# Expert rows that carry their norm, probability and token number, and a scatter from each expert tile to the output

## The chip, the cores and the metric

The kernel runs on one core of a Trainium2 chip. The metric is device time in microseconds of one execution, from the runs listed below. The core has five instruction streams that this text names as the profile does: PE (TensorE, matrix products, with PEld for its weight loads), DVE (VectorE), ACT (ScalarE), POOL (GpSimd) and SP (SyncE, which here only issues DMAs). Each stream works off its instructions in a fixed order; an instruction that waits holds up everything behind it on the same stream. SBUF is the on-chip memory of 128 partitions, PSUM the memory that matmuls write to, and HBM the memory outside.

## The reference

Four batches of 512 tokens of width 128 pass through four residual layers: `x + mamba/attention block`, `x + gelu MLP with ternary weights`, `x + mamba block`, and `x + mixture of experts`. Only the last one is touched. In it, with the layer norm of `x` as its input:

```
logits = x @ router_w + router_b
route = jax.nn.softmax(logits, axis=1)
max_prob = jnp.max(route, axis=1, keepdims=True)
max_ind = jnp.argmax(route, axis=1)
for e in range(num_experts):            # 8 experts
    h = x @ w1[e]                       # 128 -> 2 x 512
    a, g = jnp.split(h, 2, axis=1)
    y = jax.nn.silu(a) * g @ w2[e]      # 512 -> 128
    out = jnp.where((max_ind == e)[:, None], y, out)
out = out * max_prob
```

Every token thus needs one expert only, the one with the largest logit; its output is multiplied by that expert's probability and added to the token's residual.

## The kernel before

The work on a batch is cut into generators: fronts (norm, convolution, projections), scans (the state recurrences of a mamba layer, 16 jobs of two states each), `first` (attention), `dense` (two MLPs), `second` (`back1` and `route`), `sort`, `experts` and `collect`. The function `run` gives each a due time and a length, and `issue` draws one step of whichever is due next; this is the order in which the instructions are written down. A scheduler then fixes the order on each engine by its own estimate of when each is ready, and places the semaphores. Two helpers bind it further: `behind` lets something be issued only after a given instruction, and `when` adds a true dependency. A buffer tag with `bufs=n` has n buffers in rotation; a tile waits until all users of the buffer's last tile are done.

**The scans.** In `scan_states` each job makes two rows of B in PSUM (PE, L455), two decays (ACT, L459), two products and two scans (DVE, L495 and L496), and a product of 128x1024 with the loaded rows `rep` on POOL (L497); PE adds its result up in `y` (L480). The transfers `rep` go through SP's queue (L464). The instruction `self.product` is the latest of POOL's products.

**Route.** `route` (L679) normalises a batch for the experts: moments on DVE, the factor `r` on POOL (`rstd`, L292), the offset `nm_r` on DVE and the normalised rows on ACT (`shifted`, L310), which go to a tile of tag `h`. It computes logits, the one-hot choice `hot`, and the probability `top` of the chosen expert (L719).

**Sort.** Batches go through the experts in two groups, (0, 1) and (2, 3), each of 1024 tokens. `sort` (L721) counts the tokens of each expert with matmuls, and gives each token a position `posi` in an HBM buffer `sorted`, in which every expert's rows start at a multiple of 128. The buffer has 15 tiles of 128 rows, enough for any distribution, and is filled with zeros in the setup (L218 to L229). Eight indirect DMAs on POOL (L770), one for each 128 tokens, put the normalised rows there. `owni` says which expert owns each tile.

**Experts.** `experts` (L780) runs over the 15 tiles of its group. `load(j)` reads a tile `xg` from `sorted` (SP, after all eight puts), the expert's number into a register, and its weights `w_up` (512 KB, two buffers) and `w_dn` (256 KB, three) from HBM; it transposes the rows on PE (`tp`, L799) and copies them to `xj` on ACT (L801). The step of tile j then makes eight matmuls (`a_ps` L820 and `g_ps` L827), SiLU on ACT (L824) and the product on DVE (L830). `down(j - 1)` makes the four down matmuls of the previous tile (`w_ps`, L807), copies the result to `yj` on ACT (L812) and stores it through SP's queue to an HBM buffer `back` (L813). After it comes `load(j + 1)`.

**Collect.** `collect` (L841) brings one batch back in token order: four indirect DMAs on POOL gather its rows from `back` into `acc` (L848; held behind POOL's latest scan product), two POOL instructions multiply by `top` and add the residual `x` (L852 and L853), and SP stores the batch (L854). `acc` has a single buffer. Due times put the collects of batches 0 and 1 shortly after the last scan, those of 2 and 3 at the end.

Of the kernel before, what the change touches and what calls it, by code (L numbers as in the profile page):

```python
# [18 lines left out]
P = 128  # L19
# [13 lines left out]
NXR = NR + E - 1  # L33
NG = 2
SCALE = HD ** -0.5
NEG = -1e30
# [15 lines left out]
class Net:  # L52


    def __init__(self, ctx, tc, a, out):
        self.tc, self.nc, self.a, self.out = tc, tc.nc, a, out
        pool = lambda name, bufs, **k: ctx.enter_context(tc.tile_pool(name=name, bufs=bufs, **k))
        self.const = pool("const", 1)
        self.tok = pool("tok", 2)
        self.feat = pool("feat", 2)  # L60
        self.scan = pool("scan", 2)
        self.small = pool("small", 2)
        self.p_mm = pool("p_mm", 4, space=PSUM)
        self.p_b = pool("p_b", 3, space=PSUM)
        self.p_y = pool("p_y", 1, space=PSUM)
        self.dram = pool("dram", 2, space=DRAM)
        self.x = [None] * B

# [86 lines left out]
    def setup_rest(self):  # L155
# [5 lines left out]
        nc.gpsimd.tensor_copy(self.ident_b, self.ident)  # L161
        self.ones = self.c("ones", [P, P])
        nc.gpsimd.memset(self.ones, 1.0)
# [41 lines left out]
        )  # L205
        self.ones_b = self.c("ones_b", [P, P], BF16)
        nc.gpsimd.memset(self.ones_b, 1.0)
# [9 lines left out]
        )  # L217
        zero = self.big("zero", [P, NX, D])  # L218
        nc.gpsimd.memset(zero, 0.0)
        self.sorted = []  # L220
        for k, rows in enumerate(GROUPS):
            n = len(rows) * NT + E - 1
            d = self.dram.tile([n * P, D], F32, tag=f"sorted{k}", name=f"sorted{k}", bufs=1)
            for j in range(0, n, NX):
                m = min(NX, n - j)
                nc.sync.dma_start(
                    out=d[j * P:(j + m) * P, :].rearrange("(j p) d -> p j d", p=P), in_=zero[:, :m, :]
                )
            self.sorted.append(d)  # L229
# [38 lines left out]
    def ternary(self, name, raw, shape):  # L268

        nc = self.nc  # L270
        col = self.c(f"abs_{name}", [P, 1])
        nc.vector.tensor_reduce(
            col, raw, AX.X if len(shape) == 2 else AX.XY, ALU.add, apply_absolute_value=True
        )
        ps = self.mm(f"abs_ps_{name}")
        nc.tensor.matmul(ps[:, 0:1], lhsT=self.ones, rhs=col, start=True, stop=True)
        thr = self.c(f"thr_{name}", [P, 1])
        nc.vector.tensor_scalar(thr, ps[:, 0:1], 0.5 / (D * HID), 0.5e-6, ALU.mult, ALU.add)
        nthr = self.c(f"nthr_{name}", [P, 1])
        nc.vector.tensor_scalar(nthr, thr, -1.0, None, ALU.mult)  # L280
        low = self.big(f"low_{name}", shape)
        nc.vector.tensor_scalar(low, raw, nthr, None, ALU.is_lt)
        w = self.c(f"tern_{name}", shape)
        nc.vector.scalar_tensor_tensor(w, raw, thr, low, ALU.is_gt, ALU.subtract)
        return w

    def load_x(self, b):
        self.x[b] = self.tok.tile([P, NT, D], F32, tag="x", name=f"x_{b}", bufs=B)
        self.nc.sync.dma_start(out=self.x[b], in_=self.a["x"][b].rearrange("(t p) d -> p t d", p=P))


    def rstd(self, name, var, eps):  # L292
        nc = self.nc
        r = self.sm("r", [P, NT], bufs=4)
        ve = self.sm("ve", [P, NT], bufs=4)
        nc.gpsimd.tensor_scalar(ve, var, eps, None, ALU.add)
        nc.gpsimd.tensor_tensor(r, ve, self.nhalf, ALU.pow)
        return r
# [10 lines left out]

    def shifted(self, y, x, mean, r, name="nm_r"):  # L310

        nc = self.nc
        off = self.sm(name, [P, NT], bufs=4)
        nc.vector.scalar_tensor_tensor(off, mean, -1.0, r, ALU.mult, ALU.mult)
# [49 lines left out]
    def front(self, b, layer, x, scale=None):  # L364
# [53 lines left out]
        du = self.ft("du", [P, NB, T])  # L418
        v, e = self.ft("sp_v", [P, NB, T], bufs=1), self.ft("sp_e", [P, NB, T], bufs=1)
        for c in range(NB):  # L420
# [20 lines left out]
    def scan_states(self, b, layer):  # L441
# [47 lines left out]
        for k, (c, n) in enumerate(jobs):  # L489
# [4 lines left out]
            for i, b in enumerate(b_n):  # L494
                nc.vector.tensor_tensor(b, b, du[:, c, :], ALU.mult)  # L495
                nc.vector.tensor_tensor_scan(hs[:, i, :], da[:, i, :], b, 0.0, ALU.mult, ALU.add)  # L496
            self.product = nc.gpsimd.tensor_tensor(hs, hs, rep, ALU.mult)  # L497
            done[k] = hs
# [180 lines left out]
    def route(self, b):  # L679
# [4 lines left out]
        if n == 0:  # L684
            self.choice = (
                self.sm("hot", [P, NR, E], bufs=1)[:, :nr],
                self.small.tile([P, NR, E], BF16, tag="hot_b", name="hot_b", bufs=1)[:, :nr],
                self.sm("top", [P, NR])[:, :nr],
            )
        hot, hb, top = (t[:, ts] for t in self.choice)  # L690
        x = self.x[b]
        mv = self.moments("e", [x[:, t, :] for t in range(NT)])
        ln = self.shifted(self.t4("h", bufs=4), x, mv[:, :, 0], self.rstd("e", mv[:, :, 1], 1e-5))
        self.h[b] = ln
        xT = self.transposed(ln)
# [22 lines left out]
        nc.vector.tensor_reduce(sum_e, lg, AX.X, ALU.add)  # L718
        nc.vector.reciprocal(top, sum_e)  # L719

    def sort(self, group):  # L721
        nc = self.nc
        hot, hb, top = self.choice
        nr = len(group) * NT
# [4 lines left out]
        for s in range(1, nr):  # L729
            nc.tensor.matmul(  # L730
                rk[:, s:, :], lhsT=self.ones_b, rhs=hb[:, :nr - s, :], start=False, stop=(s == nr - 1)
            )
        ct = self.mm("count_ps")[:, :E]
        for t in range(nr):
            nc.tensor.matmul(ct, lhsT=self.ones_b, rhs=hb[:, t, :], start=(t == 0), stop=(t == nr - 1))

# [32 lines left out]
        for t in range(nr):  # L769
            put = nc.gpsimd.indirect_dma_start(  # L770
                out=srt, out_offset=bass.IndirectOffsetOnAxis(ap=posi[:, t:t + 1].bitcast(U32), axis=0),
                in_=self.h[group[t // NT]][:, t % NT, :], in_offset=None,
            )
# [3 lines left out]
        yield  # L777
        self.order = srt, puts, owni, posi, top

    def experts(self, group):  # L780
        nc = self.nc
        srt, puts, owni, posi, top = self.order
        nx = len(group) * NT + E - 1
        back = self.dram.tile([nx * P, D], F32, tag="back", name="back")

        def load(j):

            xg = self.ft("xg", [P, D], bufs=2)
            get = nc.sync.dma_start(out=xg, in_=srt[j * P:(j + 1) * P, :])
# [5 lines left out]
            with self.behind(self.rep):  # L795
                for part, name in zip(w, ("w1_rows", "w2_rows")):
                    nc.sync.dma_start(out=part, in_=self.a[name][bass.ds(e, 1)].rearrange("o p n -> (o p) n"))
            tp = self.mm("tp")
            nc.tensor.transpose(tp[:, :P], xg, self.ident)  # L799
            xj = self.ft("xj", [P, P])  # L800
            nc.scalar.copy(xj, tp[:, :P])  # L801
            return w, xj

        def down(j, w, sa):
            ps = self.mm("w2_ps")
            for f in range(EF // P):
# [3 lines left out]
                )  # L810
            yj = self.ft("yj", [P, D])
            nc.scalar.copy(yj, ps[:, :D])  # L812
            nc.sync.dma_start(out=back[j * P:(j + 1) * P, :], in_=yj)  # L813

        ahead, last = load(0), None
        for j in range(nx):
            w, xj = ahead
            pa = self.mm4("a_ps")
# [12 lines left out]
            if last is not None:  # L831
                down(j - 1, *last)
            last = w, sa
            if j + 1 < nx:
                ahead = load(j + 1)
            yield
        down(nx - 1, *last)
        for n, b in enumerate(group):
            self.moe[b] = back, posi[:, n * NT:(n + 1) * NT], top[:, n * NT:(n + 1) * NT]

    def collect(self, b):  # L841

        nc = self.nc
        back, posi, top = self.moe[b]
        acc = self.t4("acc", bufs=1)
        with self.behind(self.product):
            for t in range(NT):
                nc.gpsimd.indirect_dma_start(  # L848
                    out=acc[:, t, :], out_offset=None, in_=back,
                    in_offset=bass.IndirectOffsetOnAxis(ap=posi[:, t:t + 1].bitcast(U32), axis=0),  # L850
                )
        nc.gpsimd.tensor_tensor(acc, acc, top.unsqueeze(2).to_broadcast([P, NT, D]), ALU.mult)  # L852
        nc.gpsimd.tensor_tensor(acc, acc, self.x[b], ALU.add)  # L853
        nc.sync.dma_start(out=self.out[b].rearrange("(t p) d -> p t d", p=P), in_=acc)  # L854
        yield

# [13 lines left out]
    def run(self):  # L870
        self.h, self.m = [None] * B, [None] * B
        self.fronts, self.backs, self.last_head = 0, {}, None
        self.moe, self.product = [None] * B, None
        self.setup()
# [5 lines left out]
        for b in range(B):  # L880
# [6 lines left out]
            stages.append((b + B + 1, 0.1, self.second(b)))  # L887
            stages.append((2 * B + (0.2 if b in GROUPS[0] else 2), 0.1, self.collect(b)))
        for group in GROUPS:
# [5 lines left out]
def steps(g):  # L895

    return {
        "scan0": 17, "scan1": 17, "front0": 8, "front1": 8, "first": 15, "dense": 8, "second": 1,
        "sort": 1, "experts": NXR, "collect": 1, "setup_rest": 5,
    }[g.__name__]  # L900
# [70 lines left out]
```

## Time and profile before

| | us |
|---|---|
| median of 3 runs | 995.21 (995.03 to 995.97) |
| profiled execution | 998.23 |
| its span in the profile | 996.5 |

| engine | busy us of the span | share |
|---|---|---|
| PE | 806.9 | 81% |
| DVE | 654.1 | 66% |
| ACT | 563.1 | 57% |
| POOL | 455.7 | 46% |

The span runs from the first to the last event of the profile on this core. A busy share is an average over stages with different limits. Shapes are written as partitions x elements. A row of a group of instructions gives the line, the engine and operation, the names of what is written and read, then busy time and mean duration, and the idle time of the engine before it with what ended it. A row of the timeline gives start, length, engine, line, operation, names, and in brackets the engine's wait before it. Relevant sizes from the page: the 30 expert tiles (15 for each group) move 512 KB of `w_up`, 256 KB of `w_dn`, 64 KB of `xg` and 64 KB of `back` each; the 16 puts and the 16 gathers are POOL instructions of about 0.97 us each.

### The profile page before, as it was taken

What the parts mean: (1) busy time and instruction counts of PE and PEld (TensorE: products, weight loads), DVE (VectorE), ACT (ScalarE), POOL (GpSimd) and SP (SyncE); (2) the same over time, 40 slices, a digit from 0 to 9 for tenths busy, and PEclk for the clock granted to TensorE, in tenths of its full rate; (3) what the DMA queues carried; (4) which work ended last, traced back from release to release, by engine and by line L of the source; (5) the groups of instructions that cost most, each with busy time, mean ns of one, the idle gap of its engine ahead of it and who ended that gap; (6) DMA issues with size and microseconds to landing.
All of it is one profiled execution on the core that took longest, in us unless ns stands there. A gap on an engine that the chain in (4) does not pass through costs nothing. (4 is left out here: it accounts for less than half of the span.)

```text
span 996.5 us, 10318 instructions
## 1 busy us (share of the span) xinstructions
PE 806.9 (81%) x3242; PEld 451.3 (45%) x3242; DVE 654.1 (66%) x1081; ACT 563.1 (57%) x938; POOL 455.7 (46%) x294
## 2 busy tenths in 40 slices
PE   4786789997899998989989999897687979844860
PEld 1332244453444554445544456444334656523760
DVE  2499876877578665878666658765888788930110
ACT  4573356647579555876756854766455757611220
POOL 4256653644444444445443335355466444563004
PEclk9987989998899999999999959799798989976995
DMA  5244322131212131112221113112125756515751
GB/s 146 75 137 155 140 93 67 62 127 63 85 64 86 43 106 64 64 64 98 94 85 43 65 43 106 61 66 66 63 94 195 267 169 216 183 42 165 239 175 42
DMA packets 50068, 105.09 MB, mean 105 GB/s; under 512 B 6791, under 2 KB 24926, under 8 KB 50014
## 3 DMA queue, kind: packets, MB, share of 16 engines
q1 hardware_dynamic: 48990, 102.34, 30.5%
q0 software_dynamic: 1024, 2.10, 0.7%
q8 instruction: 25, 0.41, 0.2%
q14 instruction: 29, 0.24, 0.1%
HBM read 98.13 MB, written 6.29 MB: 105 GB/s over the span
## 5 line engine op out<-in xcount | busy, mean ns | idle before, releaser
L497 POOL TENSOR_TENSOR hs<-hs,rep 128x1024 f32<-128x1024 f32 x128 | 306.5, 2396 | 326.1 <-DVE hs L496 177.5
L496 DVE TENSOR_TENSOR_SCAN hs<-decay,b_n 128x512 f32<-128x512 f32 x256 | 302.7, 1207 | 3.8 <-ACT decay L459 1.8
L480 PE MATMUL y<-hs,ident 128*128 128x512 f32 x512 | 282.2, 664 | 17.4 <-POOL hs L497 17.4
L459 ACT ACTIVATE decay<-delta,nega 128x511 f32<-128x511 f32 x256 | 177.5, 717 | 120.7 <-DVE hs L496 93.3
L495 DVE TENSOR_TENSOR b_n<-b_n,du 128x512 f32<-128x512 f32 x256 | 168.0, 687 | 43.8 <-PE b_n L455 38.3
L480 PEld LDWEIGHTS y<-hs,ident 128*128 128x128 f32 x512 | 101.4, 210 | 128.3 <-issue 78.2
L455 PE MATMUL b_n<-parts,sel 128*128 128x512 bf16 x256 | 91.4, 408 | 48.3 <-DVE hs L496 43.8
L830 DVE TENSOR_TENSOR sa<-sa,g_ps 128x512 f32<-128x512 f32 x30 | 20.5, 683 | 68.0 <-PE g_ps L827 64.7
L379 PE MATMUL conv_ps<-xpad,taps 128*128 128x512 f32 x128 | 62.1, 614 | 3.1 <-ACT xpad L360 2.6
L577 ACT ACTIVATE pr<-s_ps,nm 128x128 f32<-128x128 f32 (+2 forms) x64 | 33.5, 523 | 54.0 <-DVE nm L576 53.3
L588 PEld LDWEIGHTS tp<-v,pT 128*128 128x128 f32 x320 | 44.0, 205 | 33.1 <-ACT pT L584 19.5
L568 PE MATMUL s_ps<-kT,qT 32*128 32x128 f32 (+3 forms) x128 | 55.3, 514 | 0.0
L848 POOL DMA_INDIRECT acc<-back,pos_i x16 | 15.6, 973 | 76.3 <-DMA back<-yj 66.5
L455 PEld LDWEIGHTS <-sel 128*128 128x128 bf16 x256 | 26.6, 107 | 52.7 <-issue 50.9
L588 PE MATMUL tp<-v,pT 128*128 128x33 f32 x320 | 45.9, 286 | 2.1 <-ACT pT L584 2.1
L820 PE MATMUL a_ps<-xj,w_up 128*128 128x128 f32 x240 | 35.5, 291 | 11.3 <-DMA w_up<-in_w_rows 6.6
L581 PEld LDWEIGHTS tp<-ident,pr 128*128 128x128 f32 x160 | 21.2, 152 | 50.7 <-ACT pr L577 38.7
L581 PE MATMUL tp<-ident,pr 128*128 128x128 f32 x160 | 31.7, 300 | 13.4 <-ACT pr L577 13.0
L820 PEld LDWEIGHTS a_ps<-xj,w_up 128*128 128x128 f32 x240 | 32.1, 200 | 22.4 <-ACT xj L801 13.4
L576 DVE TENSOR_REDUCE nm<-s_ps 128x1 f32<-128x128 f32 (+2 forms) x64 | 30.7, 480 | 16.9 <-PE s_ps L571 15.0
L584 ACT COPY pT<-tp 128x384 f32<-128x384 f32 (+1 forms) x48 | 24.4, 509 | 30.2 <-PE tp L581 30.0
L595 DVE RECIPROCAL rs<-tp 128x1 f32<-128x1 f32 (+1 forms) x48 | 8.0, 166 | 48.5 <-PE s_ps L571 27.5
(199 smaller groups left out, 1240.7 us busy)
## 6 DMA issues: line engine op xcount, KB each, us to landing
rep<-cd SPq DMA_DIRECT2D x128, 512.0 KB, 3.7
w_up<-in_w_rows SPq DMA_DIRECT2D x30, 512.0 KB, 4.4
w_dn<-in_w_rows SPq DMA_DIRECT2D x30, 256.0 KB, 4.2
xg<-sorted SPq DMA_DIRECT2D x30, 64.0 KB, 4.1
back<-yj SPq DMA_DIRECT2D x30, 64.0 KB, 3.4
sorted<-zero SPq DMA_DIRECT2D x2, 704.0 KB, 5.9
x<-in_x SPq DMA_DIRECT2D x4, 256.0 KB, 3.9
raw_cw<-in_cw_rows SPq DMA_DIRECT2D x2, 512.0 KB, 4.1
```

What stands on the lines that cost most here:

```text
L379: last = nc.tensor.matmul(ps, lhsT=taps[:, k, c * P:(c + 1) * P], rhs=xpad[:, k:k + T], start=(k == 0), stop=(k == KC - 1),)
L455: spread = nc.tensor.matmul(t, lhsT=self.sel[:, n + i:n + i + 1].to_broadcast([P, P]), rhs=parts, start=True, stop=True)
L459: nc.scalar.activation(da[:, i, 1:], delta[:, c, 1:], AF.Exp, scale=neg_a[:, c * NS + n + i:c * NS + n + i + 1],)
L480: nc.tensor.matmul(y[c], lhsT=self.ident, rhs=hs[:, i, :], start=False, stop=(n + i == NS - 1),)
L495: nc.vector.tensor_tensor(b, b, du[:, c, :], ALU.mult)
L496: nc.vector.tensor_tensor_scan(hs[:, i, :], da[:, i, :], b, 0.0, ALU.mult, ALU.add)
L497: self.product = nc.gpsimd.tensor_tensor(hs, hs, rep, ALU.mult)
L568: nc.tensor.matmul(ps[:, k0:k0 + nk], lhsT=qT[hp, i * P:nk], rhs=kT[hp, :nk], start=True, stop=False)
L577: nc.scalar.activation(pr[:, k0:k0 + nk], ps[:, k0:k0 + nk], AF.Exp, bias=nm[:, n:n + 1])
L581: last = nc.tensor.transpose(tp[:, j * P:(j + 1) * P], pr[:, j * P:(j + 1) * P], self.ident)
L588: nc.tensor.matmul(tp[:, n * w:(n + 1) * w], lhsT=pT[:, (at[n] + j) * P:(at[n] + j + 1) * P], rhs=v[:, j, g, :], start=(j == 0), stop=(j = ...
L820: nc.tensor.matmul(pa[:, f, :], lhsT=w[0][:, f * P:(f + 1) * P], rhs=xj, start=True, stop=True)
```

## The change

Four columns are added to every row of `x` in SBUF: `rows_x` has 132 columns, and `x` is a view of the first 128. The others hold the norm's scale (`SCL`), its offset (`OFF`), the probability (`PROB`) and the token's number as an integer (`NUM`). The number is written in the setup, the other three in `route`. `sort` puts the raw 132-column rows in place of normalised 128-column ones. The fill of `sorted` is zero, with the token number 2048, one past the last.

In `experts`, `load` normalises each tile after it is read (`xn`, ACT). `down` reads the result from PSUM on DVE, multiplies by the row's probability and adds the row's residual in one instruction, and scatters the 128 rows to the output with an indirect DMA on POOL. Rows with the number 2048 are out of bounds and are not written. `xg` has four buffers in place of two, `yj` three in place of two. The function `collect`, the buffer `back`, `top` and `self.product` are gone.

Beside that: the normalised rows of `route` use the tag `ln` in place of `h`; two tiles of ones shrink to a column (and eight columns) that matmuls read with step zero; the tile `v` of the front uses the buffer of `du` in place of one of its own.

```diff
+SCL, OFF, PROB, NUM = D, D + 1, D + 2, D + 3
+XW = D + 4
...
+        for b in range(B):
+            nc.gpsimd.iota(
+                self.rows_x[b][:, :, NUM:].bitcast(I32), pattern=[[P, NT], [0, 1]], base=b * T,
+                channel_multiplier=1,
+            )
-        zero = self.big("zero", [P, NX, D])
+        zero = self.big("zero", [P, NX, XW])
         nc.gpsimd.memset(zero, 0.0)
+        nc.gpsimd.iota(
+            zero[:, :, NUM:].bitcast(I32), pattern=[[0, NX], [0, 1]], base=B * T, channel_multiplier=0
+        )
...
-        self.x[b] = self.tok.tile([P, NT, D], F32, tag="x", name=f"x_{b}", bufs=B)
+        self.rows_x[b] = self.tok.tile([P, NT, XW], F32, tag="x", name=f"x_{b}", bufs=B)
+        self.x[b] = self.rows_x[b][:, :, :D]
...
-        v, e = self.ft("sp_v", [P, NB, T], bufs=1), self.ft("sp_e", [P, NB, T], bufs=1)
+        v, e = du, self.ft("sp_e", [P, NB, T], bufs=1)
...
-        ln = self.shifted(self.t4("h", bufs=4), x, mv[:, :, 0], self.rstd("e", mv[:, :, 1], 1e-5))
-        self.h[b] = ln
+        r = self.rstd("e", mv[:, :, 1], 1e-5, row[:, :, SCL])
+        ln = self.shifted(self.t4("ln"), x, mv[:, :, 0], r, row[:, :, OFF])
...
-        nc.vector.reciprocal(top, sum_e)
+        nc.vector.reciprocal(row[:, :, PROB], sum_e)
...
-                in_=self.h[group[t // NT]][:, t % NT, :], in_offset=None,
+                in_=self.rows_x[group[t // NT]][:, t % NT, :], in_offset=None,
...
-            xg = self.ft("xg", [P, D], bufs=2)
+            xg = self.ft("xg", [P, XW], bufs=4)
...
+            xn = self.ft("xn", [P, D])
+            nc.scalar.activation(
+                xn, xg[:, :D], AF.Identity, bias=xg[:, OFF:OFF + 1], scale=xg[:, SCL:SCL + 1]
+            )
             tp = self.mm("tp")
-            nc.tensor.transpose(tp[:, :P], xg, self.ident)
+            nc.tensor.transpose(tp[:, :P], xn, self.ident)
...
-            yj = self.ft("yj", [P, D])
-            nc.scalar.copy(yj, ps[:, :D])
-            nc.sync.dma_start(out=back[j * P:(j + 1) * P, :], in_=yj)
+            yj = self.ft("yj", [P, D], bufs=3)
+            nc.vector.scalar_tensor_tensor(
+                yj, ps[:, :D], xg[:, PROB:PROB + 1], xg[:, :D], ALU.mult, ALU.add
+            )
+            put = nc.gpsimd.indirect_dma_start(
+                out=self.flat, out_offset=bass.IndirectOffsetOnAxis(ap=xg[:, NUM:].bitcast(U32), axis=0),
+                in_=yj, in_offset=None, bounds_check=B * T - 1, oob_is_err=False,
+            )
+            for other in self.stored:
+                self.tc.declare_no_dep(put.ins, other.ins, reason="every token has a row of its own")
+            self.stored.append(put)
...
-    def collect(self, b):
...
-            stages.append((2 * B + (0.2 if b in GROUPS[0] else 2), 0.1, self.collect(b)))
```

## The prediction

> **What bounds the kernel now.** I read the busy table by stage first, because the totals of the page (PE 81%, DVE 66%) mix stages with different limits; then the chain of waits backwards from the end; then the timeline wherever the chain enters or leaves a line of the change. Busy time by window (columns: window, its length, then busy us and instruction counts of PE, PE weight load, DVE, ACT, POOL; then the granted PE clock, DMA share and GB/s):
>
> ```profile
> 765.00:880.00 115.00, 100.29 (x521) 67.08 (x521) 92.49 (x126) 72.06 (x110) 58.43 (x28) 0.97 0.57 194
> 880.00:908.00 28.00, 4.70 (x34) 3.41 (x32) 6.11 (x33) 3.75 (x7) 19.60 (x21) 0.59 0.29 91
> 908.00:940.00 32.00, 25.95 (x193) 23.62 (x193) 5.49 (x8) 9.63 (x25) 0.00 (x0) 0.88 0.73 222
> 940.00:970.00 30.00, 22.22 (x182) 20.62 (x182) 4.82 (x7) 7.31 (x21) 0.00 (x0) 1.00 0.58 187
> 970.00:998.00 28.00, 0.00 (x0) 0.00 (x0) 0.00 (x0) 0.00 (x0) 12.28 (x12) 0.57 0.15 40
> ```
>
> The reader is to see four stages. Until 880 scan and first expert group share all engines: PE 87%, DVE 80%, POOL 51%. From 880 to 908 only POOL works: the second group is sorted. From 908 to 970 only the second group's experts run, and after 970 PE, DVE and ACT do nothing at all. The chain of waits names what fills those last 28 us (start, length, piece):
>
> ```profile
> 904.97 1.06 POOL acc L852
> 906.10 1.27 POOL acc L853
> 907.39 0.40 SPq L854
> 908.08 1.92 DMA xg<-sorted
> ...
> 969.37 0.28 ACT yj L812
> 969.66 1.53 DMA back<-yj
> ...
> 975.86 2.59 DMA acc<-back,pos_i
> 978.61 1.05 POOL acc L852
> 979.73 1.27 POOL acc L853
> 981.02 2.31 DMA out<-acc
> ...
> 984.09 0.99 POOL acc L848
> ```
>
> After the last expert copy at 969.37 follow a write to HBM, four gathers, two products, a store, and the same again for the fourth batch, which waits because `acc` has one buffer. And at 907.39 the store of batch 1 stands in SP's queue ahead of the loads of the second group's rows.
>
> The sum is made against the profiled execution: 998.23 us, span 996.5. The runs' median is 995.21, 3.0 below it; I carry the difference over unchanged.
>
> **1. The end.** Removed: all of `collect`. Added: the copy of `yj` becomes one DVE instruction, then an indirect DMA. Before, 996.5 - 969.37 = 27.1 us follow the start of the last copy. After: a DVE operation 128x128 from PSUM. Rows near it: 128x64 takes 0.22 (L596), 128x512 0.69 (L495), so 0.27 as an estimate; 0.1 to POOL. The scatter of the tile before is issued at about 968.6 (its copy started at 968.26), one takes 0.97 and the next follows 0.30 later, so the last starts at 969.9, not 969.74. The row nearest to a scatter to HBM is the sorted put, 2.7 us from issue to landing in this stage (2.2 to 5.0): 972.6. Behind the last landing now (store issued at 992.98, 2.31 to land, 995.3) stand 1.2 us to the end of the span: 973.8. **-22.7**. The bounds check is in no row; 0 to +0.5 for one instruction.
>
> **2. The start of the second group.** `pos_i` is written at 893.45, but the first put starts at 895.01, behind the four gathers of batch 1 on POOL. Without them it starts at 893.6. Eight puts at 1.275 us put the last at 902.5; it lands at 905.2 and the rows' load goes at 905.3, not 908.08: -2.8. The new ACT normalisation `xn` stands between load and transpose: 0.48 (L316, same shape) and 0.1 of semaphore, +0.6. **-2.2**. Probability and offset are now needed before the puts; the reciprocal ended at 892.45, before `pos_i`, so nothing.
>
> **3. The tiles of the second group.** The fourteen starts of `a_ps` after the first go from 915.34 to 965.26: 3.84 us a tile. Undisturbed it is 3.51 (922.45 to 925.96); the rest is waiting for weights:
>
> ```profile
> 939.81 0.33 SPq L813 DMA_DIRECT2D back<-yj  x1
> 940.39 0.34 SPq L797 DMA_DIRECT2D w_up<-in_w_rows  x1
> ...
> 943.79 1.13 PE L820 MATMUL a_ps<-xj,w_up 128*128 128x128 f32 x8 [0.73 <-DMA w_up<-in_w_rows]
> ```
>
> The timeline shows why: from here on `w_up` sits in SP's queue behind `back<-yj`, which waits for the copy. That store goes. Without it 3.50 are possible: 13 x 0.34 = -4.4. But a new wait comes: `xg` is now held until the scatter of its tile has landed, and has four buffers, so the load for tile j+4 waits for scatter j. Round that ring: load L, then `xn` 0.58, transpose, copy and gaps 0.70, the tile's own step 3.50, to the end of its down matmuls in the next step and over to DVE 3.0, DVE 0.37, scatter S, 0.1 to SP: L + S + 8.3 for four tiles. With L = 2.6 (xg in 908 to 941) and S = 2.7 it is 13.6, under 4 x 3.5; with 3.4 each (xg after 938, `back<-yj` under the weight stream) 15.1, 3.77 a tile. I take 3.65: **-2.5**, ends -4.4 and +0.8 (3.9). Nothing else is queued on POOL here, and `xn` is ready under the down matmuls; uncovered it would cost the 0.58 in every tile.
>
> **4. The first group, beside the last scans.** Three engines change for each of 15 tiles: DVE +0.27, ACT -0.27 + 0.48, POOL one scatter, 0.97 + 0.30. SP loses 15 stores. The rows that decide who suffers (engine, waits for: us, times, longest):
>
> ```profile
> ACT yj L812 <- PE w_ps L807: 12.4, 6, 5.7
> PEld y L480 <- POOL hs L497: 10.7, 10, 1.8
> ```
>
> The first is a wait that ACT bears today and DVE inherits, and behind it on DVE stand the scan instructions, on which POOL and ACT wait. The second says that PE already waits for POOL's product in ten of some 28 jobs. DVE: 15 x 0.27 = 4.1, at 80% busy 3.3 on the path. POOL: a scatter in front of a product delays it by half its 1.27; 15 x 0.64 x 10/28 = 3.4. Both together 6.7, less where they fall into each other's shadow: I take **+4**, nearer to the DVE row alone. Ends: -2 (SP's queue is shorter, but PE waited for no weight here) and +15 (all of 12.4 goes to the scan, and 3.3 on top).
>
> Here a rule speaks against the change. The Trainium skill (SBUF — State Buffer, the section on its two separate sides and the one after it) says that a DMA issued from POOL has its descriptors written by POOL's cores, and that they are locked out while DVE runs in a two-port mode; it gives about 0.62 us alone and 3.1 beside such an operation, and advises SP's queue. Here eight puts ran beside a busy DVE at 730 to 740 us, in 0.95 to 1.24 each, and eight at 895 to 904 beside an idle one, in 0.96 to 1.00. By the rule 15 scatters would cost 15 x 2.48 = 37 us more, by the row at most 15 x 0.25. I go by the row.
>
> **5. Edits at or near nothing.** Five small iotas on POOL in the setup: 0.17 each (L165) and half of them before a product: **+0.3**, at most 1. `v` in `du`'s buffer: L427 writes it at 740.24, and its former reader, the scan two before, ended at 695.66; 45 us cover it. Broadcast ones: a zero-step load takes 98 ns (L455), a full one 100 (L730). `ln` in place of `h`: freed after four transposes. Rows of 528 bytes: 3% on a 64 KB load. Collects of batch 0: POOL's gathers ended at 882.55, when the moments were ready, so no gain there.
>
> **Sum**: -22.7 - 2.2 - 2.5 + 4 + 0.3 = -23.1: span 973.4, median **972.1**.
>
> **Rivals.** (B) The cover holds: first group at 0, 3.50 a tile: -22.7 - 2.2 - 4.4 + 0.3 = -29.0, **966.2**. For it: POOL is idle half of the time there. Against: DVE at 80%. (C) DVE takes over ACT's wait and the ring closes: group 0 +13, 3.9 a tile (+0.8): -10.8, **984.4**. For it: the 12.4 row. Against: the order on DVE is made anew, and the down matmuls may come before it. (D) Slower: the scatters stall POOL in the first group, each held by DVE or waiting ahead of a product; at the skill's price +37.2 for +4: -27.1 + 37.2 = +10.1, **1005.3**. It decides from 27.1 / 15 = 1.8 us per scatter on the path. Against it: puts of 0.95 to 1.24 beside DVE. The end's gain has no rival of its own: nothing is left that could run there.
>
> **Chances.** Forecast 0.50, B 0.25, C 0.17, D 0.05, elsewhere 0.03. What a measurement can tell from no change is about 0.2%, 2 us; A, B and C are all faster: 0.94, same 0.01, slower 0.05. The range 962 to 986 takes in B and C with their bounds and leaves D out.
>
> **What would show it.** Right: the last `yj` to the end of the span about 4.4 us; no PE wait for `w_up` behind a store; the rows' first load about 12 us after `pos_i`; the stage 765 to 880 longer by 4. Wrong: products on POOL waiting behind a scatter whose `yj` is not ready, DVE idle in the scan waiting for `w_ps`, PE at the transpose waiting for `xn`, or a scatter above 1.3 us.

## The result and the profile after

The changed kernel takes 988.86 us (median of 4 runs, 987.50 to 990.07); the kernel before, beside it on the same chip, 995.12. The ratio is 0.9936, with an interval of 0.9918 to 0.9954: 6 us faster, where 23 were forecast. The profiled execution took 989.92, with a span of 988.1, 8.4 below the 996.5 of before. All sums below are made between these two spans. (The profile of the kernel before is of an execution 3.1 above its median, that of the change of one 1.1 above, so the spans give 2.1 more than the medians do.)

Busy time by window, as for the kernel before, cut at the stages' new ends (window, length, then busy us and instruction counts of PE, PE weight load, DVE, ACT, POOL; granted PE clock, DMA share, GB/s):

```profile
765.00:891.00 126.00, 106.34 (x545) 70.52 (x544) 101.06 (x146) 78.60 (x111) 76.44 (x43) 0.96 0.53 173
891.00:917.00 26.00, 4.91 (x35) 3.66 (x34) 6.11 (x33) 3.74 (x7) 9.07 (x10) 0.56 0.26 81
917.00:950.00 33.00, 25.34 (x177) 22.89 (x178) 6.92 (x13) 11.29 (x24) 5.91 (x6) 0.86 0.59 196
950.00:980.00 30.00, 24.65 (x189) 22.38 (x189) 7.50 (x15) 9.97 (x22) 6.87 (x7) 0.97 0.60 179
980.00:988.00 8.00, 1.67 (x13) 1.33 (x12) 1.16 (x3) 0.00 (x0) 1.96 (x2) 0.88 0.01 0
```

The idle 28 us at the end are gone. But the stage of scans and first expert group now ends at 891 instead of 880, and the second group, from its first row load to its last `yj`, takes 65.2 us (916.5 to 981.7) where it took 61.3 (908.1 to 969.4), though nothing of the old way back is left in it. Between the two spans the terms are:

| term | forecast | measured | how |
|---|---|---|---|
| end: last `yj` to end of span | -22.7 | -20.7 | 27.15 to 6.43 |
| start of group 2: `pos_i` to first `a_ps` | -2.2 | -2.3 | 17.48 to 15.20, from the end of `pos_i` |
| tiles of group 2 | -2.5 | +3.6 | 13 x (4.12 - 3.84) |
| scans and group 1, with the setup | +4.3 | +11.1 | end of `pos_i` 893.45 to 904.53 |
| sum | -23.1 | -8.3 | (the spans: -8.4) |

The page has the new instructions among its costliest groups, and the row load among its DMA issues (the last number there is the median us from issue to landing):

```profile
L832 POOL DMA_INDIRECT out<-yj,xg x30 | 29.9, 996 | 63.0 <-DVE yj L829 60.3
L811 ACT ACTIVATE xn<-xg 128x128 f32<-128x128 f32 x30 | 14.8, 494 | 48.8 <-DMA xg<-sorted 48.6
xg<-sorted SPq DMA_DIRECT2D x30, 66.0 KB, 2.3
```

The scatter costs POOL 1.0 us, as the puts did; no sign of a scatter held up by DVE. What stands out is 48.6 us in which ACT waited for a row load.

**Where the tiles of group 2 lose.** PE stands still because `xn` is late. The first and longest of these waits is for the sort; five more, 5.5 us together, fall among the tiles:

```profile
PE tp L815 <- ACT xn L811: 22.0, 6, 16.5
```

`xn` is late because its row load is late, and the row load because it waits for its buffer, that is for the scatter of the tile four before, as the forecast had said: ten of the eleven loads that have to wait go 0.1 us after that scatter has landed. With the tiles numbered from 0, these lines show tile 7 (its row load at 944.09, `xn`, transpose, its two sets of matmuls), then `yj` and scatter of tile 6, and among them the row loads of tile 9 (952.38) and tile 10 (956.67):

```profile
944.09 0.33 SPq L801 DMA_DIRECT2D xg<-sorted  x1
...
947.04 0.49 ACT L811 ACTIVATE xn<-xg 128x128 f32<-128x128 f32 x1 [2.30 <-DMA xg<-sorted]
947.59 0.33 PE L815 MATMUL tp<-ident,xn 128*128 128x128 f32 x1 [1.69 <-ACT xn L811]
...
948.27 1.87 PE L845 MATMUL a_ps<-xj,w_up 128*128 128x128 f32 x8 [0.35 <-ACT xj L817]
...
949.94 1.91 PE L852 MATMUL g_ps<-xj,w_up 128*128 128x128 f32 x8
...
951.89 0.33 SPq L809 DMA_DIRECT2D w_up<-in_w_rows  x1
...
952.38 0.33 SPq L801 DMA_DIRECT2D xg<-sorted  x1
...
952.89 0.35 DVE L829 SCALAR_TENSOR_TENSOR yj<-w_ps,xg 128x128 f32<-128x128 f32 x1 [0.24 <-PE w_ps L824]
...
953.51 0.98 POOL L832 DMA_INDIRECT out<-yj,xg  x1 [5.97 <-DVE yj L829]
...
956.67 0.33 SPq L801 DMA_DIRECT2D xg<-sorted  x1
```

A tile's own round is as long as forecast where nothing else holds it. For tile 4: load issued at 932.37, landed 934.76; `yj` at 942.41, scatter 943.03, landed 946.71; next load into that buffer at 946.84. That is 14.5 us, 3.62 a tile. But the six rounds that start after it take 16.4 to 17.8. The reason lies in the order on PE, where the down matmuls of a tile stand behind the matmuls of the next one. So the `yj` of tile 6, and with it the buffer for tile 10, waits for the row of tile 7, whose load had itself waited for the scatter of tile 3. This round leads from load to load in three tiles and not in four: tile 4 at 932.37, tile 7 at 944.09, tile 10 at 956.67, tile 13 at 969.12. That is 11.7, 12.6 and 12.5 us, 4.08 a tile. Its parts are 2.4 to 3.1 to the row's landing, 1.3 to the tile's first matmul, 3.0 to the `yj` of the tile before (4.6 in the round shown), 0.6 to its scatter, 3.0 to 4.3 to the landing, 0.1 to the next load. The 4.6 has another cause: from 948.2 to 952.0 the granted clock was 0.55, so that tile 8 started 5.0 us after tile 7 instead of 3.5.

The row load of tile 9 stood 3.1 us longer: the scatter of tile 5 had landed at 949.26, but the load was behind the `w_up` of its own tile (951.89) in SP's queue, and that `w_up` waited for the `g_ps` matmuls of tile 7 to release its buffer. This cost nothing, since tile 9 started 3.5 us after tile 8 all the same. SP's waits for scatters over these tiles:

```profile
SPq L801 <- DMA out<-yj,xg: 9.5, 8, 2.1
```

**Where group 1 loses.** The first `xn` stands on ACT ahead of the last front's copy and cast (L418, L424), and the eight puts have not landed yet:

```profile
744.90 0.49 ACT L811 ACTIVATE xn<-xg 128x128 f32<-128x128 f32 x1 [7.98 <-DMA xg<-sorted]
745.42 0.58 ACT L418 COPY crow<-bc_ps 16x512 f32<-16x512 f32 x1
746.02 0.59 ACT L424 CAST parts<-bc_ps 128x512 bf16<-128x512 f32 x1
746.64 0.70 DVE L425 TENSOR_TENSOR rest<-bc_ps,parts 64x512 f32<-64x512 f32 x1 [7.67 <-ACT parts L424]
```

DVE stands idle for 7.67 us behind the cast. In the kernel before the same cast started 9.4 us earlier:

```profile
736.63 0.58 ACT L410 CAST parts<-bc_ps 128x512 bf16<-128x512 f32 x1
```

Later in this stage SP waits for scatters, with the scans' `rep` loads queued behind (740 to 890). ACT then stands at seven more `xn`, 13.4 us together, and POOL once for a `rep`, 2.3 us:

```profile
SPq L801 <- DMA out<-yj,xg: 35.6, 9, 5.5
```

The wait that the forecast had feared, DVE's for the down matmuls, came to 4.8 us there, not 12.4.

**The end.** The chain of waits of the changed kernel:

```profile
977.48 0.98 POOL out L832
978.46 2.53 issue
981.11 0.12 issue
981.22 0.98 POOL out L832
982.20 1.29 POOLq L973
```

The last scatter starts at 982.51 and lands at 984.60. SP's closing waits are done at 985.20; POOL's closing drain (L973, issued at 982.10) ends at 987.33 and 0.8 us of bookkeeping follow. So POOL holds the end for 2.1 us after SP. Before, that drain ended at 995.66, at SP's 995.73.

### The profile page after: what moved, and what is told of

It reads as the page before. It is cut to its first block, busy times and chain, and to the rows that moved or that the text cites. A ratio compares the mean times of both kernels' runs of the same rounds, so it can differ in the third digit from the quotient of the medians.

```text
span 988.1 us, 10337 instructions
## 1 busy us (share of the span) xinstructions
PE 807.4 (82%) x3242; PEld 450.1 (46%) x3242; DVE 660.1 (67%) x1111; ACT 572.1 (58%) x938; POOL 460.1 (47%) x305
## 5 line engine op out<-in xcount | busy, mean ns | idle before, releaser
L832 POOL DMA_INDIRECT out<-yj,xg x30 | 29.9, 996 | 63.0 <-DVE yj L829 60.3
L369 PE MATMUL tp<-ident,ln 128*128 128x128 f32 x96 | 25.0, 335 | 37.5 <-ACT ln L330 20.8
L369 PEld LDWEIGHTS tp<-ident,ln 128*128 128x128 f32 x96 | 14.3, 160 | 66.1 <-ACT ln L330 22.3
L811 ACT ACTIVATE xn<-xg 128x128 f32<-128x128 f32 x30 | 14.8, 494 | 48.8 <-DMA xg<-sorted 48.6
L595 PE MATMUL tp<-ident,pr 128*128 128x128 f32 x160 | 32.0, 303 | 13.0 <-ACT pr L591 12.5
```

The lines of the kernel that those rows point to most:

```text
L369: nc.tensor.transpose(ps[:, t * P:(t + 1) * P], x[:, t, :], self.ident)
L595: last = nc.tensor.transpose(tp[:, j * P:(j + 1) * P], pr[:, j * P:(j + 1) * P], self.ident)
L832: put = nc.gpsimd.indirect_dma_start(out=self.flat, out_offset=bass.IndirectOffsetOnAxis(ap=xg[:, NUM:].bitcast(U32), axis=0), in_=yj, in_ ...
```

## The experiments

**Theory T**: three new waits took the gain. (a) The ring of four `xg` buffers holds SP and ACT; (b) the first `xn` stands on ACT ahead of the front while the puts land; (c) POOL's drain lost its cover. **Rival R1**: the loss beside the scans is the added work itself (a DVE operation and a scatter for each tile). The landmarks of all profiles, each from one trace; "scans end" is the end of the last product on POOL. Each ratio is to the kernel before in runs on the same chip (medians 994.90 to 995.83):

| kernel | median us | ratio (interval) | scans end | us a tile, group 2 | last `yj` to end |
|---|---|---|---|---|---|
| before | 995.12 | 1 | 875.9 | 3.84 | 27.15 |
| the change | 988.86 | 0.9936 (0.9918 to 0.9954) | 887.1 | 4.12 | 6.43 |
| eight `xg` | 977.78 | 0.9830 (0.9814 to 0.9846) | 884.7 | 3.52 | 6.43 |
| first `xn` held | 983.87 | 0.9887 (0.9870 to 0.9904) | 878.7 | 3.86 | 6.44 |
| both | 970.74 | 0.9761 (0.9747 to 0.9774) | 873.4 | 3.53 | 6.44 |
| rows and `xn`, old way back | 1002.89 | 1.0078 (1.0060 to 1.0096) | 881.8 | 3.78 | 26.96 |
| held, five `xg` | 971.28 | 0.9756 (0.9732 to 0.9780) | 875.4 | 3.51 | 6.43 |
| held, six `xg` | 972.29 | 0.9769 (0.9743 to 0.9794) | 876.8 | 3.53 | 6.43 |
| both, last tile by SP | 968.98 | 0.9726 (0.9700 to 0.9752) | 875.5 | 3.57 | 5.07 |
| held, six, work twice | 974.14 | 0.9787 (0.9762 to 0.9812) | 876.1 | 3.57 | 7.66 |
| both, early drain | 969.78 | 0.9743 (0.9724 to 0.9762) | 877.3 | 3.52 | 4.36 |
| the same on another chip | 967.91 | 0.9722 (0.9701 to 0.9744) | 877.2 | 3.51 | 4.36 |
| early drain, held longer | 970.14 | 0.9747 (0.9724 to 0.9769) | 880.5 | 3.48 | 4.36 |

"Scans end" resolves about 2 to 3 us: profiles of the kernels with equal code up to 700 us already stand up to 2.8 apart at 500.

**Eight buffers.**

```diff
-            xg = self.ft("xg", [P, XW], bufs=4)
+            xg = self.ft("xg", [P, XW], bufs=8)
```

> The changed kernel with eight buffers for xg instead of four. Theory T (the ring of four buffers makes SP's row loads wait for the landing of old scatters, and the normalisation xn on ACT wait for the loads): the tiles of the second group go from 4.12 us to about 3.55 (-7.4), and in the first group SP's waits for scatters (35.6 us in the stretch 740 to 890) go and bring some -3; about 978.5. Rival R1 (the first group loses through the added work itself, a DVE operation and a scatter per tile): the tail gains the same, the first group stays about 10 later than in the kernel before; about 981.5. Rival R2 (the tiles of the second group are slow because loads, scatters and weights share the DMA engines, not because of the buffers): 4.1 us a tile as before the edit, about 988.

977.78. The tiles went to 3.46 us for most, 3.52 in the mean: 13 x 0.60 = 7.8 of the 11.1 gained. R2 is out. The rest lies before: the scans end 2.5 earlier; between 703 and 900 us they gain 4.4 on the changed kernel, 1.9 of it a lag that they had at 703. SP's wait for scatters from 740 to 890 fell from 35.6 to 13.6 us; ACT's seven later waits for a row and POOL's for a `rep` are gone. The first `xn` waits as before:

```profile
ACT xn L811 <- DMA xg<-sorted: 8.0, 1, 8.0
DVE rest L425 <- ACT parts L424: 7.6, 1, 7.6
```

**First `xn` held behind the front's cast.**

```diff
-        nc.scalar.copy(parts, ps)
+        self.cast = nc.scalar.copy(parts, ps)
...
-            nc.scalar.activation(
+            norm = nc.scalar.activation(
...
+            if group is GROUPS[0] and j == 0:
+                self.when(self.cast, norm)
```

> The changed kernel with the first group's first xn held back until the last front's cast of parts is done on ACT; four buffers as before. T: the 8.0 us that ACT stood at the first xn with the front's copy and cast behind it go; the end of the last scans comes about 5 earlier, the tail stays 4.1 us a tile: about 984. R1: the wait was slack, and nothing changes: about 988.

983.87: -5.0. Its timeline:

```profile
735.50 0.59 ACT L424 CAST parts<-bc_ps 128x512 bf16<-128x512 f32 x1
736.45 0.69 DVE L425 TENSOR_TENSOR rest<-bc_ps,parts 64x512 f32<-64x512 f32 x1
...
742.60 0.88 ACT L811 ACTIVATE xn<-xg 128x128 f32<-128x128 f32 x2 [6.51 <-DMA xg<-sorted]
```

The cast comes at once, and `xn` waits behind it. From 703 to 777 us the scans gain 5 on the changed kernel. (The profile caught the fastest of the five runs, six below the median. Its 3.86 a tile shows how far the four-buffer ring varies, not a gain of the edit, and the end of its scans, 8.4 earlier, is more than the medians allow.)

**Both.**

> Both edits: eight buffers and the first xn held back. T: the gains add, about 974, scans' end within 4 of the kernel before. R1: as with eight buffers alone, about 981.5.

970.74, 2 below the sum of the two gains, and the scans end 2.5 earlier than in the kernel before. The two edits together undo the loss beside the scans, with every added DVE operation and scatter still in place: R1 can't explain it. Whether they undo all of it is less sure: this profile lies 2.4 below its median and that of the kernel before 3.1 above. By the medians the gain is 24.3 and not the 30.1 between the spans; if the difference lies in the scans, some 3 us of their loss (13 by the medians) are left. In the second group ACT no longer waits: of SP's waits there only this is left of the ring (905 to 966):

```profile
SPq L801 <- DMA out<-yj,xg: 2.9, 6, 0.8
```

**Rows and `xn` alone.** The change without its way back: `down` copies on ACT and stores to `back`, `collect` gathers as in the kernel before, with the probability from the rows.

```diff
-            nc.vector.scalar_tensor_tensor(
-                yj, ps[:, :D], xg[:, PROB:PROB + 1], xg[:, :D], ALU.mult, ALU.add
-            )
-            put = nc.gpsimd.indirect_dma_start(
...
+            nc.scalar.copy(yj, ps[:, :D])
+            nc.sync.dma_start(out=back[j * P:(j + 1) * P, :], in_=yj)
```

> Half of the change: rows of 132 columns and xn on ACT, but the way back as in the kernel before (ACT copy, store to back, gathers, product and sum per batch). T: the first xn still stands ahead of the front's instructions and waits for the puts, so that the scans end 5 to 8 later than in the kernel before; end of the kernel as before: about 1001. R1 (added DVE operation and scatter are the cost): the scans end about 1 later, about 996.5.

1002.89, with scans that end 5.9 later than in the kernel before, though none of the work that R1 names is there. Its waits from 740 to 890:

```profile
ACT xn L812 <- DMA xg<-sorted: 8.5, 1, 8.5
DVE rest L425 <- ACT parts L424: 8.2, 1, 8.2
```

**How many buffers.** With the first `xn` held, five and six in place of eight.

> First xn held back and five buffers for xg. T: one round of the ring took 4 x 4.12 = 16.5 us with four buffers; five tiles at 3.46 give it 17.3, so nearly all waits go: about 3.5 us a tile in the second group, total within 1.5 of the kernel with eight buffers, about 971.5. Rival (the rounds are longer than the mean says, the longest landings decide): 3.7 a tile, about 975.

> First xn held back and six buffers for xg. T: as with eight in the tiles (3.46 us each), and the first tile of the second group starts some 0.5 earlier, because fewer row loads are queued ahead of its weights: about 970.5. Rival (the first group needs more than six): scans end 2 to 4 later than with eight, about 974.

971.28 and 972.29, not to be told from eight. Five already cut the ring: its round of 11.7 to 12.6 us then leads over four tiles, 3.1 a tile, less than the 3.46 that a tile takes anyway. The half microsecond at the start of the second group did not come: `pos_i` to `a_ps` is 14.9 with five, six and eight.

**The work of the way back twice.** In the first group alone, on six buffers:

```diff
+            if group is GROUPS[0]:
+                y2 = self.ft("y2", [P, D], bufs=3)
+                nc.vector.scalar_tensor_tensor(
+                    y2, ps[:, :D], xg[:, PROB:PROB + 1], xg[:, :D], ALU.mult, ALU.add
+                )
+                twin = nc.gpsimd.indirect_dma_start(
+                    out=self.aside, out_offset=bass.IndirectOffsetOnAxis(ap=xg[:, NUM:].bitcast(U32), axis=0),
+                    in_=y2, in_offset=None, bounds_check=B * T - 1, oob_is_err=False,
+                )
```

> Six buffers, first xn held back, and in the first group alone each tile's DVE operation and POOL scatter are done twice (the second into a buffer of its own): the added work of the way back doubled beside the scans. T (that work lies beside other work once xg and xn don't wait): 0 to 3 later than with six buffers and single work. R1 (15 DVE operations and 15 scatters take the scans' time): 6.7 later by the working of the prediction. A scatter that DVE holds up at the skill's price: 37 later.

974.14, 1.9 more, of which the end took 1.2 (7.66 for 6.43, see below). The scans end where they did. All 30 scatters of that stage are about as short as alone, 1.10 at most:

```profile
L834 POOL DMA_INDIRECT out<-yj,xg x15 | 15.1, 1008 | 8.0 <-DVE y L843 3.3 <-DVE yj L831 2.9 <-issue 0.9
L846 POOL DMA_INDIRECT aside<-y,xg x15 | 14.6, 975 | 4.6 <-issue 2.7 <-DVE hs L510 0.9 <-DVE b_n L509 0.6
```

Meanwhile DVE was busy for 124 of 150 us (740 to 890). What the added work costs beside the scans is too small to see; and no scatter here shows the price that the Trainium skill (SBUF — State Buffer, the sections named in the prediction) gives for a DMA that POOL issues beside a two-port DVE operation. DVE's time here goes to `TENSOR_TENSOR`, scans and `SCALAR_TENSOR_TENSOR`; whether any of them runs in that mode the traces don't tell, so the case shows only that scatters beside this work pay no such price.

**The end.** The last tile of the second group is stored by SP instead, to a buffer of its own, so that its rows are missing from the output:

```diff
+            if group is GROUPS[-1] and j == nx - 1:
+                nc.sync.dma_start(out=self.dram.tile([P, D], F32, tag="aside", name="aside", bufs=1), in_=yj)
+                return
```

> Eight buffers, first xn held back, and the very last tile of the second group is stored by SP as plain rows into a buffer of its own instead of being scattered to the output: the rows of that tile are left out of the output. T (POOL's own closing drain, which ends 2.7 us after its last transfer, has lost its cover of an SP store): the last yj to the end of the span goes from 6.44 to about 4.2, so about 968.5. Rival (the end is the landing of the last transfer, whoever issues it): 6.4 stays within 0.5, about 970.7.

5.07, between the two expectations. The drain did not shrink to 2.7 after the transfer before; it ended 3.76 after POOL's last instruction. Laid beside the other traces this shows what it follows (times in us, read from the traces):

```
kernel                    indirect DMAs  POOL's last ends  drain ends  between
before                         32            992.95          995.66     2.70
rows and xn, old way back      32            998.39         1001.11     2.71
both, last tile by SP          45            963.06          966.82     3.76
the change                     46            983.49          987.33     3.84
both                           46            961.80          965.64     3.84
held, six, work twice          61            965.16          970.23     5.07
```

From 32 to 61 it is 2.37 / 29 = 0.082 us for each indirect DMA (of 128 rows, all of them) that POOL has issued, and 0.09 besides; 45 and 46 lie on this line. So a second drain, behind the second group's puts where POOL is idle, should pay part of it early:

```diff
             puts.append(put)
+        if group is GROUPS[-1]:
+            self.tc.keep_in_program_order(nc.gpsimd.drain())
         yield
```

> Eight buffers, first xn held back, and one more drain on POOL behind the eight puts of the second group. In the runs so far the closing drain ends 2.70 us after POOL's last instruction where POOL issued 32 indirect DMAs, 3.76 at 45, 3.84 at 46 and 5.07 at 61, which is 0.08 us for each. If the drain pays for the indirect DMAs since the last drain, the early one pays for 31 where POOL is idle, the closing one for 15 (1.3 us), SP's closing waits end last, and the last yj to the end of the span goes from 6.44 to about 4.3: about 968.5. Rival (it pays for all of the program, or a drain in the middle clears nothing): 6.4 stays, about 970.7, and the early drain only lies in POOL's idle time.

It does: the early drain ends 2.64 after the last put (31 x 0.082 + 0.09 = 2.6), the closing one 1.76 after the last scatter, level with SP's closing waits, and the last `yj` to the end takes 4.36, in this and two further profiles of the same kernel (the first of these is a single run of 971.83). For the 15 scatters since the early drain the line gives 1.3, not 1.76; what holds the last half microsecond is open. The runs:

> The same kernel once more, for a second profile: the same end of the span as in the first within 0.1 us.

> The kernel with the early drain once more, on the same chip as the one before, to compare with: about 969.8.

By medians the 2.1 us are at the edge of what the intervals tell apart (0.9743 and 0.9722 against 0.9761 without the early drain).

**Held longer.** The first `xn` behind the last front's logarithm (L445) instead of its cast:

> As with the early drain, but the first xn of the first group is held back further, until the last front's logarithm on ACT is done; with the hold at the cast ACT still stood 6.2 to 6.5 us at this xn, with decays and the front's four activations behind it. T (what is queued behind a waiting xn is what the scans lose): the last front's delta comes some 4 us earlier and the scans end 2 to 4 earlier than with the early drain alone, about 967. Rival (that wait was slack, the scans are held by DVE and POOL there): the same within 1, about 969.8.

A miss: 970.14 against 967.91 for the shorter hold on the same chip (their intervals overlap); the scans ended 3 later, not 2 to 4 earlier. The rival, no change, fits better. Most of the 6 us for which ACT still stood at `xn` was slack: the front's logarithm came 11.4 us after the cast instead of 13.2, with decays in between that wait 2.4 and 2.6 us for DVE's scans. Up to 823 us the scans gained 0.7 by it, and between there and 843 they lost 2.9, where the order of later instructions is another; that was not followed further. So T(b) holds for the cast that stood behind `xn`, not for everything on ACT behind it.

## Why the prediction was wrong in size

The forecast sum of -23.1 missed the measured -8.3 by 14.8: 6.8 in the first group, 6.1 in the tiles of the second, 2.0 at the end. The steps for the first two failed; at the end one term was mis-sized.

**1. The end** (-22.7, measured -20.7). The mechanism was right. The term of 1.2 us between the last landing and the end of the span took in SP's closing work only; POOL's drain had been just as long beside it, and with 46 indirect DMAs for 32 and no store of SP behind, it holds the end, 3.5 us behind the last landing (+2.3). The last scatter started 0.8 after the last `yj`, not 0.5 (+0.3), and landed in 2.1, not 2.7 (-0.6).

**2. The start of the second group** (-2.2, measured -2.3). Right, by its own steps: the rows' first load 12.2 after `pos_i` began, and 0.58 for `xn`.

**3. The tiles** (-2.5, measured +3.6). The stall behind `back<-yj` went as said. The step that failed is the ring: it was named, and the fixed part of 8.3 was right for a tile that nothing else holds (8.4 measured), but it was summed as a round of four tiles in which the next tile always starts on time ("the tile's own step 3.50"). The next tile's row is in the same ring. `yj` of a tile waits for it on PE, and the round is then one of three tiles, without the 3.50: 11.7 to 12.6 measured, 4.08 a tile. The scatter's landing was a little mis-sized besides (3.0 to 4.3 in that round, for 2.7 to 3.4), and 1.5 us came from the low clock at one tile. Five buffers give 3.51, the 3.50 that the forecast had as its best end. That buffers are what was short, the runs with eight, six and five show; the three-tile round is read from the trace, and no run changed the order on PE to test it.

**4. The first group** (+4; with the setup +4.3, measured +11.1). The reasons were wrong, and this step failed too: it took `xn` on ACT as work ("-0.27 + 0.48") and put its wait at nothing. DVE's and POOL's added work costs next to nothing (doubled: scans' end unmoved). What costs is `xn` as a wait: the forecast checked that `xn` is ready in the second group and priced it by 0.58, but did not ask what stands behind the first `xn` on ACT while the puts land (about 5 us), nor what stands on ACT and in SP's queue behind a row that waits for a scatter (about 4, counted from 703 us on). The upper bound of +15 covered it, but by another wait, which is luck. How much of each is the wait itself, and how much the new order of instructions that each edit brings with it, was not separated.

**5. The small edits.** What the iotas cost can't be told. At 112 us, after thirteen of POOL's products, the changed kernel is 1.5 us behind the kernel before; in the twelve other profiles with the same setup it is between -0.3 and +1.3. The forecast's 0.3, at most 1, lies within.

Of the rivals, C (984.4) came nearest, and half by its mechanism: the ring did close, while DVE did not take over ACT's wait (4.8 of 12.4). Scatters held up on POOL (D) did not come. Of the forecast's own signs of being wrong one came, PE at the transpose waiting for `xn`. The change's own gain was there to be had: with five to eight buffers and one hold it is 24 us by the medians. That this is near the forecast's -23.1 is in part chance, since the end gave less than forecast and the tiles more.

## What to carry to other kernels

When a buffer's last reader moves from early in a tile (a transpose) to its very end (a scatter's landing), count the buffers anew, and follow the ring through the order on every engine that it passes, not as a chain by itself: where a tile's result stands behind the next tile's work, that tile's row is part of the round, and four buffers carry it over three tiles. For every new instruction that waits for a transfer, ask what stands behind it on its engine at the first tile, where the data are latest, and not in the steady state alone. Whatever a removed stage covered at the end of the program (here a drain) comes to light with it.

## What the hardware showed

POOL's drain took 0.082 us for each indirect DMA that POOL had issued since the last drain, 2.7 us at 32 and 5.1 at 61, long after those transfers had landed (in the kernel before, the last of them landed 5.25 us before the drain's end). A drain where POOL is idle takes that part off the end: 6.44 to 4.36. Besides, eight matmuls of one late tile took 1.91 us instead of 1.06, at a granted clock of 0.55 (948.2 to 952.0) between stretches at 1.00; whether the 1.69 us stop before it caused that was not tried, and stops of 1.13 and 1.32 us passed without it (1.00 from 935.3 to 939.0 and from 969.7 to 973.5).
